# Expert parts with their last three tiles behind a branch, and parts of 3, 3 and 2 blocks behind attention

## The chip, the cores and the metric

The kernel runs on one core of one Trainium2 chip. A core has five engines that run side by side, each through its own instruction queue in order: TensorE (PE, matrix products), VectorE (DVE), ScalarE (ACT), GpSimd (POOL) and SyncE (SP, which here issues transfers). Engines wait for one another by semaphores. On-chip memory is SBUF, with PSUM as the target of matrix products; transfers between it and the large memory (HBM) are done by DMA, issued from the queues of SP, ACT and POOL.

The metric is the device time of one execution in microseconds (us). Before the change it is 656.89 us, the median of three runs (655.76 to 658.45).

## The reference

The input x is 16 sequences of 256 tokens with 128 features, float32. The layer is a feed-forward half, attention, and the same feed-forward half again:

```python
x = x + 0.5 * ffn(layernorm(x))
x = x + attention(layernorm(x))     # 16 heads of 8, causal
x = x + 0.5 * ffn(layernorm(x))
```

The feed-forward part is a mixture of experts. A token takes the two best of eight experts by a softmax over `layernorm(x) @ gate_w.T`, with the two weights scaled to sum to one. The reference computes every expert for every token and weights the unused ones with zero:

```python
weights, idx = top_k(softmax(flat @ gate_w.T), 2)
h1 = einsum("nd,ehd->neh", flat, w1); h3 = einsum("nd,ehd->neh", flat, w3)
y = einsum("neh,edh->ned", silu(h1) * h3, w2)     # 8 experts, 256 hidden units
out = einsum("ned,ne->nd", y, combine)
```

## The kernel before

**Blocks, parts and tiles.** The 4096 tokens are 8 blocks of 512, and a block is two sequences. Each feed-forward half is cut into three parts of whole blocks: 1, 3 and 4 blocks before attention (`ahead`), and 4, 3 and 1 behind it (`after`). The rows that a part sends to experts are sorted by expert into a scratch array in HBM (`part.x`), with every expert's rows starting at a multiple of 128. A tile is 128 such rows, all of one expert. A part of `blocks` blocks has `8 * blocks` tiles' worth of rows, and rounding up eight experts can add at most 7, so the kernel always works through `nj = 2 * ht + NE - 1` tiles, which is 15, 23, 31 or 39 for 1, 2, 3 or 4 blocks. That is 85 tiles before attention and 85 behind it. Tiles that hold no row are computed all the same. Three scratch pairs (`places`), for 1, 3 and 4 blocks, are used by both halves.

**Routing** (`route_in_steps`) finds on VectorE, from the gate's logits, the two experts of each token, counts tokens for each expert by a small matrix product, and yields the row of each token (`rowi`, L416), the expert of each tile (`eji`, L434), and the weights `c`. It is written as a generator, whose steps the caller spreads between other work.

**Scatter and gather.** `scatter` (L449) writes normalised rows to `part.x` with indirect DMAs from POOL, two for 128 tokens, so 8 for a block. `combine` (L611) reads the results back from `part.y` with as many indirect DMAs from POOL, and VectorE adds each to x (L602), at most some four transfers later. When a block is complete behind attention, SP stores it (`store`).

**The tile loop** (`experts`). For each group of three tiles SP loads rows (`xg`), two groups ahead, with three buffers; PE transposes them (`px`, L493), and ACT copies them to SBUF (`xgT`, L495). For each tile VectorE copies the expert's weights to a fixed place (`wt`, L502), two tiles ahead, by an address in a register that was loaded from `eji`. PE then makes four products to `ph` (L514), ACT applies silu (L525), VectorE multiplies (L536), and two tiles later PE makes two products to `py` (L544). For each group ACT copies `py` to `yg` (L554) and issues its store to `part.y`.

**The order of the work** is written out by hand: within `manual_schedule` each engine gets its instructions in program order. `experts_of` runs the tiles of one part. At every tile it takes `pulls` steps from `aside` (work on PE, ACT and VectorE that belongs to something else) and, from tile 2 on, `rate` steps from `beside` (scatters or gathers), each behind a small POOL memset called `tick`. When all tiles are begun it exhausts `aside`, with `ahead` also `beside`, and then fetches and begins the next part (its first loads, transposes and weight copies), before the last products of its own part. At the end it exhausts `beside`.

- Before attention: part one runs beside the scatters of part two and the norms, gates and routing of part three; part two beside the scatters of part three; part three beside the gathers of parts one and two and, from tile 14 on, the opening steps of attention.
- In attention, each batch (sequence) has eight steps `p`. At each, one step is taken from `moves`: first the gathers of the last part ahead (one in two steps), then the scatters of whichever part behind attention has been routed. When a sequence is finished, `finish` projects it and adds it to x, and after every second one normalises the block and computes its logits. With the last block of a part the routing follows, and its scatters join `moves`. In the last batch the first part behind attention begins, with five tiles (silu by tanh there).
- Behind attention: part one runs beside the rest of the scatters, and takes the rest of `finish` and the routing one step a tile (`ending`); part two beside the gathers of part one (one a tile); part three beside the gathers of part two (four in three tiles); and at last the gathers of part three.

Of the kernel before, what the change touches and what calls it, by code (L numbers as in the profile page):

```python
# [11 lines left out]
FP = mybir.dt.float32  # L12
BF = mybir.dt.bfloat16
I32 = mybir.dt.int32
AF = mybir.ActivationFunctionType
ALU = mybir.AluOpType
# [3 lines left out]
P = 128  # L20
NB, SEQ, D = 16, 256, 128
NH, DK = 16, 8
NE, NHID = 8, 256
# [12 lines left out]
HT = NT // 2  # L36
JG = 3
NJG = 13


class InTurn:
# [9 lines left out]
class Part:  # L51


    def __init__(self, first, blocks, scratch):
        self.first, self.blocks = first, blocks
        self.ht = blocks * TPB


        self.nj = 2 * self.ht + NE - 1
        self.ng = -(-self.nj // JG)  # L60
        self.x, self.y = scratch


MASKED = -1e30
# [3 lines left out]
def macaron_kernel(  # L68
# [41 lines left out]
    def load_x(*blocks):  # L110
        for t in blocks:
            nc.sync.dma_start(
                out=xs[t], in_=x[ts(t, BLK), :].rearrange("(c p) d -> p c d", p=P)
            )


    def scratch(name, blocks):
        rows = Part(0, blocks, (None, None)).nj * P
        return tuple(tc.dram_tile([rows, D], FP, name=f"{name}_{s}") for s in "xy")

    places = [scratch(f"rows{i}", n) for i, n in enumerate((1, 3, 4))]
    ZW = 16
    zeros = const.tile([P, ZW * D], FP)
    nc.vector.memset(zeros, 0.0)

    def clear(i, queue=nc.sync):
        rows = places[i][0].rearrange("(p c) d -> p (c d)", p=P)
        n = rows.shape[1]
        for at in range(0, n, ZW * D):
            w = min(ZW * D, n - at)  # L130
            queue.dma_start(out=rows[:, at : at + w], in_=zeros[:, 0:w])
# [1 line left out]
    gw_sb = const.tile([D, NE], FP)  # L133
    nc.scalar.dma_start(out=gw_sb, in_=gate_w)
    load_x(0, 1)
    clear(0)
    load_x(2, 3)
    w13_sb = const.tile([D, NE, 2, NHID], FP)
    w2_sb = const.tile([P, NHC, NE, D], FP)
# [4 lines left out]
    nc.sync.dma_start(out=w2_sb, in_=w2)  # L144
    clear(1)
    load_x(4, 5, 6, 7)
    wq_in = const.tile([D, NG, 4, 32], FP)
    wk_in = const.tile([D, NG, 4, 32], FP)
    wv_sb = const.tile([D, D], FP)
# [33 lines left out]
    nc.vector.memset(zero8, 0.0)  # L183

    goes_on = {}
    for blocks in (1, 3, 4):
        n = blocks * TPB
        go = const.tile([P, NE, n], FP, tag=f"goes_on{n}", name=f"goes_on{n}")
        nc.gpsimd.memset(go.rearrange("p e t -> p (e t)"), 1.0)
        nc.gpsimd.memset(go[:, :, 0], 0.0)  # L190
        goes_on[n] = go.rearrange("p e t -> p (e t)")
# [138 lines left out]
    def route_in_steps(part, ps, fine=False, placed_at=None):  # L330
# [86 lines left out]
        if placed_at is not None:  # L417
            placed_at(rowi)
        yield

        grid = [1, part.ng * 4, NE]
        past = work.tile([1, NJG * 4, NE], FP, tag="g_past", name="past")[:, 0 : part.ng * 4, :]
        nc.vector.tensor_tensor(
            past,
            jgrid[:, 0 : part.ng * 4, :],
            upto[0:1, :].unsqueeze(1).to_broadcast(grid),
            ALU.is_ge,
        )
        if fine:
            yield  # L430
        ej = work.tile([1, NJG * 4], FP, tag="g_ej", name="ej")[:, 0 : part.ng * 4]
        nc.vector.tensor_reduce(ej, past, AX.X, ALU.add)
        eji = work.tile([1, NJG * 4], I32, tag="g_eji", name="eji", bufs=3)
        nc.vector.tensor_scalar(eji[:, 0 : part.ng * 4], ej, float(NE - 1), None, ALU.min)  # L434

        den = new("den", [P, ht])
        nc.vector.tensor_scalar(den, ex, 2.0, 2.0, ALU.mult, ALU.add)
# [28 lines left out]
    def experts(part, eji):  # L466
# [71 lines left out]
        def project(j):  # L538
# [12 lines left out]
            if c == tiles(g) - 1:  # L551
# [7 lines left out]
                    in_=yg[:, 0:n, :],  # L559
                )  # L560

        def fetch():
            load(0)
            load(1)
# [23 lines left out]
                    project(j - 2)  # L588
                yield

        made = SimpleNamespace(part=part, fetch=fetch, begin=begin, tiles=run(), begun=False, by_tanh=False)
        return made


# [60 lines left out]
    def experts_of(  # L655
        work,
        beside,
        aside=iter(()),
        side=(0, 0),
        pulls=lambda j: 1,  # L660
        rate=lambda j: 1,
        then=None,
        opened=None,
        ahead=True,
    ):

        following = None

        def transfer():
            nc.gpsimd.memset(tick, 0.0)  # L674
            return next(beside, done)

        done = object()
        with opened or ExitStack() as stack:
            one = 1 if side[1] else 2
            if opened is None:  # L680
                banks = expert_banks(stack, one, 3 if side[1] else 4)
            else:
                banks = work.banks
                more = psum(stack, "ps_h2", 2)
                banks.h = InTurn(banks.h, more)
            if side[0]:
                pools["first"], pools["banks"] = psum(stack, "ps_f", 1), side[0]
            if side[1]:
                pools["side"] = psum(stack, "ps_m", side[1])
            stack.enter_context(manual())  # L690
            if not work.begun:
                work.fetch()
                work.begin(banks)
            work.banks = banks
            for _ in work.tiles:
                j = work.at
                for _ in range(pulls(j)):
                    next(aside, None)
                for _ in range(rate(j) if j >= 2 else 0):
                    transfer()  # L700
                if j == work.part.nj:
                    for _ in aside:
                        pass
                    while ahead and transfer() is not done:
                        pass
                    if then is not None:
                        following = then()
                        following.fetch()
                        following.begin(banks)
            while transfer() is not done:  # L710
                pass
        return following

# [319 lines left out]
        return opening, steps, routes, moves  # L1033

    ahead = [Part(0, 1, places[0]), Part(1, 3, places[1]), Part(4, 4, places[2])]
    after = [Part(0, 4, places[2]), Part(4, 3, places[1]), Part(7, 1, places[0])]


    stats, xns, xnTs, routes = {}, {}, {}, []
# [124 lines left out]
    def others():  # L1164
        part = ahead[2]
        blocks = range(part.first, part.first + part.blocks)
        for s in range(part.blocks + 2):
            t = part.first + s
            if t in blocks:
                normed(t)  # L1170
            if t + 2 in blocks:
                stats[t + 2] = moments(t + 2)
            if t - 1 in blocks:
                xnTs[t - 1] = transposed(t - 1, xns[t - 1], pools["side"])
            if t - 2 in blocks:
                gate_logits(t - 2, xnTs[t - 2], pools["side"])
            if s == part.blocks:
                clear(2, nc.scalar)
            yield
        routes.append((yield from route_in_steps(part, pools["side"])))  # L1180

# [10 lines left out]
    def back(part, route, after_block):  # L1192
        return combine(part, route[0], route[2], after_block)

    def store(t):
# [24 lines left out]
        itertools.chain(back(ahead[0], routes[0], none), back(ahead[1], routes[1], none)),  # L1220
        opening(),
        (2, 1),
        pulls=lambda j: int(j >= 14),
    )

    left, right = ExitStack(), ExitStack()
# [20 lines left out]
    with manual():  # L1247
# [10 lines left out]
        then=lambda: experts(after[1], left_routes[1][1]),  # L1258
        opened=opened,
    )  # L1260
    tiles = experts_of(
        tiles,
        back(after[0], left_routes[0], store),
        then=lambda: experts(after[2], left_routes[2][1]),
        ahead=False,
    )
    experts_of(
        tiles,
        back(after[1], left_routes[1], store),
        rate=lambda j: 1 + (j % 3 == 0),  # L1270
        ahead=False,
    )
    for _ in back(after[2], left_routes[2], store):
# [41 lines left out]
```

## Time and profile before

| | us |
|---|---|
| median of three runs | 656.89 |
| the profiled execution's own time | 657.1 |
| its span | 655.1 |
| PE busy | 576.9 (88%) |
| DVE busy | 448.2 (68%) |
| POOL busy | 419.7 (64%) |
| ACT busy | 352.7 (54%) |
| `ph` products (L514), 1360 records | 184.9 |
| `py` products (L544), 680 records | 104.6 |
| scatters (L449), 128 | 126.5 |
| gathers (L611), 128 | 124.9 |

The span is the time from the first to the last instruction of one profiled execution, and all times in a profile are counted from its start. A profile lists groups of instructions by line, with busy time, the mean of one in ns, and the idle time of the engine just before them with what ended it ("<-"). "issue" there is time in which the engine waited for nothing that the profile shows, such as the loading of registers. PE is a matrix product and PEld the load of its weights. The chain of work is followed back from the last instruction, at each step to what released it.

### The profile page before, as it was taken

What the parts mean: (1) busy time and instruction counts of PE and PEld (TensorE: products, weight loads), DVE (VectorE), ACT (ScalarE), POOL (GpSimd) and SP (SyncE); (2) the same over time, 40 slices, a digit from 0 to 9 for tenths busy, and PEclk for the clock granted to TensorE, in tenths of its full rate; (3) what the DMA queues carried; (4) which work ended last, traced back from release to release, by engine and by line L of the source; (5) the groups of instructions that cost most, each with busy time, mean ns of one, the idle gap of its engine ahead of it and who ended that gap; (6) DMA issues with size and microseconds to landing.
All of it is one profiled execution on the core that took longest, in us unless ns stands there. A gap on an engine that the chain in (4) does not pass through costs nothing.

```text
span 655.1 us, 17006 instructions
## 1 busy us (share of the span) xinstructions
PE 576.9 (88%) x6158; PEld 484.4 (74%) x6158; DVE 448.2 (68%) x1405; ACT 352.7 (54%) x730; POOL 419.7 (64%) x862
## 2 busy tenths in 40 slices
PE   4369799999998999999999999999998799999930
PEld 3258699999986677777777766777677799999930
DVE  7754765566665788888887899677646556576742
ACT  6245444446623667777686866675646345444410
POOL 3568889767532666666663437788710884787785
PEclk9989999999996999999999999999999979999985
DMA  8726444454310000000000000000112333456442
GB/s 301 276 86 225 131 125 130 134 137 107 78 42 20 19 14 20 18 18 15 18 18 3 2 2 23 29 30 36 58 38 60 110 110 94 131 148 165 122 121 72
DMA packets 65905, 53.73 MB, mean 82 GB/s; under 512 B 6560, under 2 KB 60576, under 8 KB 65312
## 3 DMA queue, kind: packets, MB, share of 16 engines
q1 hardware_dynamic: 34368, 22.16, 10.8%
q0 software_dynamic: 8192, 16.79, 8.6%
q10 hardware_dynamic: 23264, 13.71, 7.1%
q8 instruction: 50, 0.82, 0.5%
q14 instruction: 31, 0.25, 0.1%
HBM read 25.43 MB, written 27.20 MB: 80 GB/s over the span
## 4 chain that ended last, share of the span: by engine, by line
PE 70%; POOL 8%; DVE 8%; issue 5%; ACT 5%; DMA 2%; DVEq 1%; ACTq 0%; POOLq 0%; SPq 0%
PE ph L514 18%; PE sm L782 12%; PE py L544 8%; PE o L887 7%; PE sw L797 6%; PE sm L809 6%; POOL rows_x L449 4%; PE pl L315 3%; POOL yt L611 3%; PE px L493 2%; PE pt L302 2%; DVE top L813 2%; ACT pT L823 1%; PE pm L868 1%; PE po L925 1%
## 5 line engine op out<-in xcount | busy, mean ns | idle before, releaser
L514 PE MATMUL ph<-xgT,wt 128*128 128x128 f32 x1360 | 184.9, 280 | 8.6 <-DVE wt L502 6.7
L514 PEld LDWEIGHTS ph<-xgT,wt 128*128 128x128 f32 x1360 | 169.3, 196 | 11.7 <-DVE wt L502 5.5
L825 POOL TENSOR_SCALAR_AFFINE_SELECT pT<-pT 128x256 f32<-128x256 f32 x256 | 100.0, 414 | 107.4 <-ACT pT L823 106.3
L813 DVE TENSOR_REDUCE top<-sm 128x3 f32<-128x384 f32 x256 | 130.3, 551 | 54.5 <-PE sm L809 51.4
L449 POOL DMA_INDIRECT rows_x<-xn,rowi x128 | 126.5, 988 | 47.7 <-issue 22.6
L823 ACT ACTIVATE pT<-sw 128x768 f32<-128x768 f32 x128 | 104.0, 812 | 86.2 <-PE sw L797 79.3
L611 POOL DMA_INDIRECT yt<-rows_y,rowi x128 | 124.9, 975 | 28.4 <-issue 15.9
L782 PE MATMUL sm<-kp,qp 32*128 32x256 f32 (+1 forms) x1024 | 127.9, 354 | 3.2 <-ACT kp L758 1.6
L525 ACT ACTIVATE gt<-ph 128x256 f32<-128x256 f32 x165 | 63.2, 384 | 117.4 <-PE ph L514 108.1
L797 PE MATMUL sw<-qm,kp 32*128 32x128 f32 (+1 forms) x1024 | 120.9, 354 | 1.1 <-ACT pT L823 1.1
L782 PEld LDWEIGHTS sm<-kp,qp 32*128 32x128 f32 x1024 | 95.1, 187 | 31.3 <-DVE top L813 10.6
L536 DVE TENSOR_TENSOR gt<-gt,ph 128x256 f32<-128x256 f32 x165 | 68.6, 416 | 59.9 <-ACT gt L525 59.2
L544 PE MATMUL py<-w_sb,gt 128*128 x680 | 104.6, 278 | 3.3 <-ACT yg L554 1.9
L502 DVE COPY wt<-w_sb 128x512 f32 x170 | 75.7, 448 | 36.1 <-issue 25.0
L544 PEld LDWEIGHTS py<-w_sb,gt 128*128 128x128 f32 x680 | 90.5, 194 | 4.1 <-ACT yg L554 2.3
L797 PEld LDWEIGHTS sw<-qm,kp 32*128 32x128 f32 x1024 | 68.6, 189 | 2.8 <-ACT pT L823 1.8
L602 DVE SCALAR_TENSOR_TENSOR x<-yt,c,x 128x128 f32<-128x128 f32 x128 | 45.7, 361 | 18.3 <-DMA yt<-rows_y,rowi 18.0
L887 PE MATMUL o<-pT,vaug 128*32 128x256 f32 (+1 forms) x1024 | 56.2, 335 | 0.0
L809 PE MATMUL sm<-mask_two,ident_b 128*128 128x256 bf16 x256 | 50.8, 281 | 0.0
L250 POOL TENSOR_TENSOR rstd<-ve,neg_half 128x4 f32<-128x4 f32 x24 | 25.3, 1054 | 39.6 <-DVE ve L248 38.7
L887 PEld LDWEIGHTS o<-pT,vaug 128*32 128x32 f32 x1024 | 27.7, 110 | 23.2 <-issue 9.6
L674 POOL MEMSET tick<- 128x1 f32 x269 | 37.3, 139 | 5.7
(124 smaller groups left out, 660.3 us busy)
## 6 DMA issues: line engine op xcount, KB each, us to landing
xg<-rows_x SPq DMA_DIRECT2D x56, 192.0 KB, 2.9
rows_y<-yg ACTq DMA_DIRECT2D x56, 192.0 KB, 2.1
w_sb<-in_w SPq DMA_DIRECT2D x3, 1024.0 KB
x<-in_x SPq DMA_DIRECT2D x8, 256.0 KB, 13.8
rows_x<-xn,rowi POOLq DMA_INDIRECT x128
rows_x<-zeros ACTq DMA_DIRECT2D x2, 1024.0 KB
yt<-rows_y,rowi POOLq DMA_INDIRECT x128
out_y<-x SPq DMA_DIRECT2D x8, 256.0 KB, 3.5
```

Of the source, the lines that this page charges most:

```text
L449: i = nc.gpsimd.indirect_dma_start(out=part.x, out_offset=bass.IndirectOffsetOnAxis(ap=rowi[:, n, t : t + 1], axis=0), in_=xns[part.first ...
L502: nc.vector.tensor_copy(wt.rearrange("d k h -> d (k h)"), w13_f[:, bass.ds(es[g][c] * (2 * NHID), 2 * NHID)],)
L514: nc.tensor.matmul(out=ph[:, k // NHC, k % NHC, :], lhsT=wt[:, k, :], rhs=xTs[g][:, c, :], start=True, stop=True,)
L544: nc.tensor.matmul(out=ys[g][:, c, :], lhsT=gt[:, hc, :], rhs=w2_f[:, bass.ds(es[g][c] * D + hc * (NE * D), D)], start=(hc == 0), stop=(hc ...
L611: nc.gpsimd.indirect_dma_start(out=yt, out_offset=None, in_=part.y, in_offset=bass.IndirectOffsetOnAxis(ap=rowi[:, n, t : t + 1], axis=0),)
L782: nc.tensor.matmul(out=s[u][:, to], lhsT=qp[r, j, ts(q, P)], rhs=kp[r, SET[j], k], start=(q == 1), stop=False,)
L797: nc.tensor.matmul(out=s[:, u, to], lhsT=kp[r, SET[j], ts(k, P)], rhs=qm[r, j, q], start=True, stop=True,)
L809: nc.tensor.matmul(out=s[u][:, 128:384], lhsT=ident_b, rhs=mask_qk, start=False, stop=True)
L813: nc.vector.tensor_reduce(tops[b % 2][:, j, i0 + u, :], s[u][:, 0:384].rearrange("p (n k) -> p n k", k=P), AX.X, ALU.max,)
L823: nc.scalar.activation(pT, s[:, :, 0:384], AF.Exp, scale=DK**-0.5)
L825: nc.gpsimd.affine_select(out=pT[:, u, 0:256].rearrange("p (n q) -> p n q", q=P), in_=pT[:, u, 0:256].rearrange("p (n q) -> p n q", q=P), ...
L887: nc.tensor.matmul(out=o[32 * i : 32 * i + 32, j // 2, q], lhsT=va[:, kt, 4 * j + i, :], rhs=pTs[i // 2][:, i % 2, at], start=(j % 2 == 0 ...
```

## The change

A part now always computes `nj = most - 3` tiles, where `most` is the former bound: 12, 20, 28 and 36 for 1, 2, 3 and 4 blocks. The three remaining tiles stand in `rest`, behind a branch. Every engine loads the number of tiles that the routing counted into a register, and the body is entered only if it exceeds `nj`. The body does load, transposes, products and store of three tiles one after the other. It stands behind all other tiles of its part, so behind the first loads, transposes and weight copies of the next one. What the three tiles' rows of `part.y` hold otherwise are zeros, which four new transfers from SP write near the start.

Behind attention the parts have 3, 3 and 2 blocks in place of 4, 3 and 1. So the scratch for one block becomes one for two, and a further transfer on ACT's queue clears its rest. Before attention there are now 12 + 28 + 36 = 76 tiles outside branches, and behind it 28 + 28 + 20 = 76.

Three constants follow: the opening of attention is taken from tile 11 on, the gathers beside the last part are five in four tiles, and gathers of the first part that are left when the second part's tiles end are carried on beside the third part.

```diff
@@ class Part
-        self.nj = 2 * self.ht + NE - 1
+        self.most = 2 * self.ht + NE - 1
+        self.nj = self.most - SPARE
         self.ng = -(-self.nj // JG)
+        self.grid = -(-self.most // JG)
+        self.x, self.y = (s[: self.most * P] if s is not None else None for s in scratch)
@@ macaron_kernel
-    places = [scratch(f"rows{i}", n) for i, n in enumerate((1, 3, 4))]
+    places = [scratch(f"rows{i}", n) for i, n in enumerate((2, 3, 4))]
...
-    clear(0)
+    clear(0, upto=at_first)
...
     load_x(4, 5, 6, 7)
+    for part in (Part(0, n, places[i]) for i, n in ((0, 1), (0, 2), (1, 3), (2, 4))):
+        nc.sync.dma_start(
+            out=part.y[part.nj * P :, :].rearrange("(p c) d -> p c d", p=P),
+            in_=zeros[:, 0 : SPARE * D],
+        )
...
-    for blocks in (1, 3, 4):
+    for blocks in (1, 2, 3, 4):
@@ route_in_steps
+        nc.vector.tensor_copy(eji[:, NJG * 4 : NJG * 4 + 1], upto[0:1, NE - 1 : NE])
@@ experts
+        def rest():
+            counted = nc.values_load(
+                eji[0:1, NJG * 4 : NJG * 4 + 1],
+                min_val=0,
+                max_val=part.most,
+                skip_runtime_bounds_check_because="tiles are counted by the routing",
+            )
+            banks = made.banks
+            few = range(part.nj, part.most)
+            rows = slice(part.nj * P, part.most * P)
+            with tc.If(counted > part.nj):
+                xg = work.tile([P, JG, D], FP, tag="xg", name="xg", bufs=3)
+                nc.sync.dma_start(
+                    out=xg, in_=part.x[rows, :].rearrange("(c p) d -> p c d", p=P)
+                )
+                px = banks.x.tile([P, JG, P], FP, tag="x", name="px")
+                for c in range(SPARE):
+                    nc.tensor.transpose(px[:, c, :], xg[:, c, :], ident)
+                xT = work.tile([D, JG, P], FP, tag="xgT", name="xgT", bufs=2)
+                nc.scalar.copy(xT, px)
+                wt = work.tile([D, SPARE, 2 * NHC, P], FP, tag="w_rest", name="w_rest", bufs=1)
+                py = banks.y.tile([P, JG, D], FP, tag="y", name="py")
+                for c, j in enumerate(few):
...
+                yg = work.tile([P, JG, D], FP, tag="yg", name="yg", bufs=3)
+                nc.scalar.copy(yg, py)
+                nc.scalar.dma_start(
+                    out=part.y[rows, :].rearrange("(c p) d -> p c d", p=P), in_=yg
+                )
@@ experts_of
-            while transfer() is not done:
+            work.rest()
+            while all_of_them and transfer() is not done:
                 pass
@@ the parts
-    after = [Part(0, 4, places[2]), Part(4, 3, places[1]), Part(7, 1, places[0])]
+    after = [Part(0, 3, places[1]), Part(3, 3, places[2]), Part(6, 2, places[0])]
@@ others
                 clear(2, nc.scalar)
+                clear(0, nc.scalar, since=at_first)
@@ the calls of experts_of
-        pulls=lambda j: int(j >= 14),
+        pulls=lambda j: int(j >= 11),
...
+    gathers = back(after[0], left_routes[0], store)
     tiles = experts_of(
         tiles,
-        back(after[0], left_routes[0], store),
+        gathers,
         then=lambda: experts(after[2], left_routes[2][1]),
         ahead=False,
+        all_of_them=False,
     )
     experts_of(
         tiles,
-        back(after[1], left_routes[1], store),
-        rate=lambda j: 1 + (j % 3 == 0),
+        itertools.chain(gathers, back(after[1], left_routes[1], store)),
+        rate=lambda j: 1 + (j % 4 == 0),
         ahead=False,
     )
```

## The prediction

> **What bounds the kernel now.** I read the page's chain of work first, then the busy time by stretch, then the timelines of POOL, PE and DVE around the ends of the parts. The chain by engine:
>
> ```profile
> PE 70%; POOL 8%; DVE 8%; issue 5%; ACT 5%; DMA 2%; DVEq 1%; ACTq 0%; POOLq 0%; SPq 0%
> ```
>
> TensorE carries it, and POOL only in places. The stretches say where (PE busy, count, PEld, DVE, ACT, POOL, then granted clock, DMA share, GB/s):
>
> ```profile
> 34.00:79.00 45.00, 35.20 (x248) 31.22 (x248) 26.23 (x105) 22.73 (x50) 33.85 (x70) 0.96 0.41 140
> 79.00:125.00 46.00, 45.28 (x402) 45.01 (x403) 26.64 (x90) 20.87 (x53) 40.03 (x107) 1.00 0.44 133
> 125.00:205.00 80.00, 76.87 (x636) 71.23 (x636) 51.85 (x151) 38.80 (x95) 41.04 (x88) 0.97 0.33 88
> 205.00:475.00 270.00, 265.18 (x3588) 190.99 (x3586) 215.68 (x621) 182.72 (x343) 171.84 (x323) 0.99 0.07 20
> 475.00:556.00 81.00, 71.89 (x623) 67.03 (x623) 46.72 (x163) 40.04 (x83) 40.55 (x86) 0.95 0.27 83
> 618.00:655.00 37.00, 10.27 (x90) 9.89 (x88) 13.99 (x41) 4.55 (x11) 26.11 (x44) 0.70 0.36 96
> ```
>
> PE is nearly full from 79 to 618 us, has holes before 79 and from 475 to 556, and does little in the last 37 us, where POOL's gathers run alone. POOL's timeline gives the tail its joints:
>
> ```profile
> 119.58 5.72 POOL L674 MEMSET tick<- 128x1 f32 x33
> ...
> 506.93 1.03 POOL L449 DMA_INDIRECT rows_x<-xn,rowi  x1 [14.66 <-DVE rowi L416]
> ...
> 548.64 1.35 POOL L449 DMA_INDIRECT rows_x<-xn,rowi  x1 [7.19 <-ACT yg L554]
> ...
> 563.87 1.06 POOL L611 DMA_INDIRECT yt<-rows_y,rowi  x1 [1.59 <-DMA xg<-rows_x]
> ...
> 609.42 1.04 POOL L611 DMA_INDIRECT yt<-rows_y,rowi  x1 [2.50 <-DVE wt L502]
> ...
> 648.57 0.95 POOL L611 DMA_INDIRECT yt<-rows_y,rowi  x1 [0.30 <-issue]
> ```
>
> Scatters of the 3-block part start at 506.9, those of the last block at 548.6, the 64 gathers at 563.9; the 33rd, first of the second part, waits until 609.4 for its rows. Then 32 follow without a hole, (648.57-609.42)/31 = 1.26 us each, and the span ends 6.5 us after the last starts.
>
> **What a tile costs.** L514 and L544 leave 8, 4 and (L493) 1 matmul records per tile. Between 79 and 124 us a group of three tiles takes 4.35 us, so 1.45 us each. The work removed is 170 - 152 = 18 tiles, 26 us of PE if nothing else sets the pace. Routing the reference's own inputs (top two of eight, counts divided by 128 and rounded up) gives 12, 27 and 35 tiles for the parts before attention against bounds of 12, 28 and 36, and 28, 28 and 19 against 28, 28 and 20 behind it. No branch should be entered; three counts lie on the bound.
>
> **Before attention.** Part one, 15 to 12 tiles: its PE work ends near 76, but the next part's ph starts at 79.1, released by POOL's 24th scatter (72.0 plus its 1 us), 2.2 us of landing and a 3.2 us load. Scatters run 1.27 us apart from 50 us whatever PE does: gain 0. Part two, 31 to 28: the 32 scatters of the next part fill POOL from 76.1 to 119.6, and this wait already stands in front of the next part:
>
> ```profile
> 124.30 0.55 PE L493 MATMUL px<-ident,xg 128*128 128x128 f32 x3 [0.63 <-DMA xg<-rows_x]
> ```
>
> PE would come 4.35 us sooner and wait as much longer. Fewer idle ticks on POOL may give 1 us, a register load there takes it: 0. Part three, 39 to 36, holds attention's opening, one step a tile over 25 tiles both before (from tile 14) and after (from 11). The eight rows of block 0 are added by 142.5 us, its moments start at 147.0; three tiles earlier is 142.6. It just fits: 3 x 1.45 = 4.3 us gained, 0 if those adds come late.
>
> Small additions: four 192 KB stores of zeros on SP, by ACT's issue row (0.37 us) 1.5 us, stand before the first xg load, which waits for scatters until 31 us; one more clear on ACT (0.4 us, in a stretch where ACT is half idle); two POOL memsets (0.3 us, before a 2.3 us wait); six copies of 0.17 us on DVE. 0 each, and at most 2 us together if that cover were gone.
>
> **Attention.** The second part is now complete after block 5, so its routing and 9 of its 24 scatters move inside; 8 scatters of the first part leave. DVE gains some 6 us of short operations where it is busy 216 of 270 us: 0, at worst +3.
>
> **Behind attention.** Steps for the last block are taken one a tile. Before, eight routing steps of the 3-block part went first (tiles 5 to 12), and the last block's began with the reciprocal at 509.9; after, they begin at tile 5, near 495.7: 14.2 us sooner. Its rstd also stood behind twelve scatters on POOL:
>
> ```profile
> 523.20 0.16 DVE L255 SCALAR_TENSOR_TENSOR less<-mv,rstd 128x4 f32<-128x4 f32 x1 [4.93 <-POOL rstd L250]
> ...
> 547.73 0.17 DVE L416 CAST rowi<-rows 128x8 int32<-128x8 f32 x1
> ```
>
> With part of these scatters inside attention I take 1 of the 4.9 us as left. So rowi comes at 547.9 - 14.2 - 3.9 = 530. Then 16 scatters, not 8: 16 x 1.27 = 20 us, POOL free at 550.5 (before 558.9), first gather 551.5.
>
> PE: 23 tiles from 494.6 at 1.45 = 33.3, plus 8.4 of the 14.3 us of extra work and stalls that the 34 tiles had (3.9 of rstd and 2 of one pair of exp table loads go): 536.3, first ph of the second part 538 and a branch. Its adds on DVE wait for the gathers from tile 7 on: gate 27 stands behind add 20, 551.5 + 20 x 1.26 + 3.3 = 580, so its last product is at 582.5 and its rows land at 585.5 (copy 0.5, issue 0.4, landing 2.1). POOL, done with 24 gathers at 582, waits until 586. The third part: ph at 585 with branch and start, 20 x 1.45 to 614, landed 618; POOL's 24 gathers end at 616. The last 16 start at 619 with the branch, the last at 619 + 15 x 1.26 = 637.8, end 644.3: 10.8 us sooner. The gain is smaller than PE's because 16 rather than 8 gathers now follow the last tile, 10 us more.
>
> **The branch.** No row shows one. Each needs a register on every engine, then the joining of counts behind it. Queued behind it on PE are the next part's ph, on DVE wt and gt, on ACT gt and xgT, on SP the third load, on POOL the next transfers. Nearest row: registers for three tiles before a weight copy,
>
> ```profile
> L502 DVE COPY wt<-w_sb 128x512 f32 x170 | 75.7, 448 | 36.1 <-issue 25.0
> ```
>
> 25.0 us over 38 waits, 0.66 each. Low end 0.5 us, as PE's queue hides part. High end: the join also waits for a store and a load in flight, 0.7 + 2.1 + 2.9 = 5.7. A gain is excluded, since it only adds. I take 1.5, one register load and one hand-over between PE and ACT (0.6 to 0.8), near the low end. Six places, the last counted 1.0: 8.5 us, of which 4.5 lie before attention and 4.0 are in the tail's joints.
>
> Here a rule of the Trainium skill speaks against the change: "Runtime: NRT & Kernel Launch", section "Instruction fetch mechanics", says that a taken branch whose target is outside the two fetched blocks of 256 instructions stalls for a fetch. The row:
>
> ```profile
> q8 instruction: 50, 0.82, 0.5%
> ```
>
> 0.82 MB / 50 is 16.4 KB a packet, as that page has it, but no branch is in the trace. The longest body, PE's, has 3 x 13 matmuls with as many loads, about 90 instructions: one block ahead at most. I charge nothing; if each jump did refetch, at about the 2.9 us of an xg load, six would add 17 us and the sum would end slower, at 664.
>
> **Sum.** 655.1 - 4.3 + 4.5 - 10.8 = 644.5 us of span. The profiled execution took 657.1, 2.0 above its span; the median of the runs is 656.9. So 646.4, called 646.
>
> **Rivals.**
> Cheap joins: all six at 0.5 give 646.4 - 5.5 = 641, and rstd without a stall 640. For it: PE's gaps marked issue are 0.3 to 0.6 us. Against: the buffers used in the branch rotate into the next part.
> POOL takes it back: if the last block's steps are not sooner (rowi still at 548), 16 scatters end at 568.5, the last of 64 gathers starts 63 x 1.26 = 79.4 after the first, and the end is 568.5 + 1 + 79.4 + 6.5 + 0.2 (from before attention) = 655.6, median 657: no change. For it: the steps wait on three engines at 2.1 us a tile. Against: the eight steps ahead of them are gone by the order of the code.
> The join drains: each branch waits for DMAs in flight. Without branches the sum is 636.0, so 19.1 us are to be lost: from 3.2 us a branch it is slower. At 5.7 the span is 670, median 672. For it: a store of y is in flight at every branch. Against: it is awaited by later gathers only, if the counts are joined engine by engine.
> The branch is entered: load, transposes, three tiles in series and the store, some 12 us each. The counts exclude it unless a token flips at a bound; the nearest count below a multiple of 128, where the total is on its bound, is 124: four tokens to spare.
>
> **Chances.** As forecast (639 to 653) 0.56; cheap joins 0.12; POOL takes it back 0.12; the join drains 0.18; entered 0.02. The range 638 to 664 leaves out some 0.05 below and 0.12 above; that of the likeliest alone is 639 to 653. A change under 0.5% (3.3 us) can't be told from none: faster 0.68, same 0.12, slower 0.20.
>
> **What would show it.** ph count 1216 in place of 1360; ph of part two near 79 to 81 and of part three near 125 to 127 (no gain there); rowi of the last part some 35 us after the first tile behind attention, with 16 scatters directly behind it; POOL holes of some 4 and 2 us before the gathers of parts two and three; 16 gathers behind the last tile. At each branch a PE hole under 2 us. Holes of 3 us or more, or gathers that start after 565, make the prediction wrong.

## The result, and the profile after

The changed kernel takes 664.37 us, the median of four runs (662.46 to 665.02), against 656.49 for the kernel before beside it (655.76 to 658.45). The ratio is 1.010, with a 95% interval of 1.006 to 1.014: slower by 1%, where 646 and faster were forecast. The profiled execution took 664.98, 1.7 us more than its span of 663.3.

The chain of work of the changed kernel breaks off near its end, so it can't be set beside the one shown of before:

```profile
DMA 2%; issue 1%; POOL 1%; DVE 0%; POOLq 0%; DVEq 0%
```

The busy times by stretch can. Those of the changed kernel (columns as before the change: PE busy, count, PEld, DVE, ACT, POOL, granted clock, DMA share, GB/s):

```profile
34.00:79.00 45.00, 31.70 (x214) 28.26 (x215) 25.57 (x107) 19.52 (x44) 36.67 (x70) 0.93 0.45 158
79.00:125.00 46.00, 43.95 (x373) 43.79 (x372) 24.27 (x86) 20.87 (x50) 39.10 (x104) 0.95 0.41 125
125.00:205.00 80.00, 76.31 (x599) 68.01 (x598) 48.98 (x146) 36.38 (x88) 37.13 (x71) 0.93 0.28 76
205.00:475.00 270.00, 262.15 (x3542) 188.61 (x3542) 217.14 (x647) 178.99 (x338) 165.06 (x315) 0.99 0.06 19
475.00:556.00 81.00, 73.08 (x597) 63.30 (x596) 40.75 (x130) 37.87 (x81) 43.94 (x92) 0.89 0.26 78
618.00:663.00 45.00, 12.32 (x105) 11.69 (x103) 16.41 (x48) 5.57 (x14) 31.59 (x47) 0.66 0.34 94
```

Up to 475 us little differs. From 475 to 556 PE counts as busier than before, 73.08 against 71.89 us, and yet works off fewer products (597 against 623) at a lower clock (0.89 against 0.95). So the loss is near the end of attention. The products `o`, weights times values, are the last of each of its batches. Their row has shortest, median and longest duration in ns, then first and last start. Before:

```profile
L887 PE MATMUL o<-pT,vaug x1024: 272/379/637, 209.7 to 493.0; 128*32 128x256 f32 x86, 128*32 128x128 f32 x85
```

After:

```profile
L966 PE MATMUL o<-pT,vaug x1024: 272/379/637, 207.4 to 505.6; 128*32 128x128 f32 x86, 128*32 128x256 f32 x85
```

This cuts the difference of the two spans into three. Attention's first `o` comes 2.3 us sooner; from its first `o` to its last it takes 298.2 us in place of 283.3, 14.9 more; from the last `o` to the end it is 663.3 - 505.6 = 157.7 in place of 655.1 - 493.0 = 162.1, 4.4 less. -2.3 + 14.9 - 4.4 = 8.2, the difference of the spans. So the stretch of attention, which the forecast put at nothing, lost about twice what the rest gained. (A second profile of the kernel before has its `o` from 211.6 to 493.4 us, so a joint of one profile can move by 2 us.)

POOL's timeline in the last batch (start, duration, engine and line, then the idle time before it and what ended it) shows why:

```profile
464.40 0.77 POOL L904 TENSOR_SCALAR_AFFINE_SELECT pT<-pT 128x256 f32<-128x256 f32 x2 [1.15 <-ACT pT L902]
466.99 1.02 POOL L462 DMA_INDIRECT rows_x<-xn,rowi  x1 [1.82 <-DVE rowi L426]
468.02 0.12 POOL L752 MEMSET tick<- 128x1 f32 x1
468.32 0.97 POOL L462 DMA_INDIRECT rows_x<-xn,rowi  x1 [0.18 <-issue]
469.29 0.12 POOL L752 MEMSET tick<- 128x1 f32 x1
469.60 0.97 POOL L462 DMA_INDIRECT rows_x<-xn,rowi  x1 [0.19 <-issue]
470.56 0.12 POOL L752 MEMSET tick<- 128x1 f32 x1
470.87 0.97 POOL L462 DMA_INDIRECT rows_x<-xn,rowi  x1 [0.19 <-issue]
471.85 0.78 POOL L904 TENSOR_SCALAR_AFFINE_SELECT pT<-pT 128x256 f32<-128x256 f32 x2
```

L904 is the select that masks attention's weights `pT`, and PE's `o` needs it. Four scatters stand between two pairs of selects that follow one another in attention. The ticks tell whose they are: the tile loop behind attention sets one for each of its scatters (`transfer` in `experts_of`), attention's own have none. (The tick of the first of the four had run already, before attention.) In program order these scatters come after every select of attention. But here the order written out by hand held only within one region of it (one `manual_schedule`). Attention is one region, the tile loop behind it is another, and the scatters needed nothing but `rowi` of the second part, which now exists at 466.5 because blocks 3 to 5 are complete by then. From 466.99 to 481.9 POOL took eight scatters of the later loop, four, three and one of them, ahead of three pairs of selects that PE waits for. In PE's timeline:

```profile
472.33 1.84 PE L966 MATMUL o<-pT,vaug 128*32 128x256 f32 x12 [4.07 <-POOL pT L904]
479.15 1.42 PE L966 MATMUL o<-pT,vaug 128*32 128x256 f32 x4 [0.75 <-POOL pT L904]
482.37 1.84 PE L966 MATMUL o<-pT,vaug 128*32 128x256 f32 x12 [1.80 <-POOL pT L904]
```

After the first of these waits TensorE's products are slower, too. From 472 to 492 us the granted clock is 0.51, and 76 products are worked off; with the eight scatters held back (below) it is 1.00 there, and there are 184. Eight products `sw` of attention, in the changed kernel and then with the scatters held back:

```profile
474.10 1.65 PE L876 MATMUL sw<-qm,kp 32*128 32x128 f32 x8
```

```profile
482.15 0.92 PE L880 MATMUL sw<-qm,kp 32*128 32x128 f32 x8
```

Behind attention POOL's timeline has these joints, in the changed kernel:

```profile
541.27 0.97 POOL L462 DMA_INDIRECT rows_x<-xn,rowi  x1 [10.16 <-DVE rowi L426]
...
563.94 0.98 POOL L688 DMA_INDIRECT yt<-rows_y,rowi  x1 [1.20 <-issue]
...
603.84 1.14 POOL L688 DMA_INDIRECT yt<-rows_y,rowi  x1 [8.65 <-DVE gt L549]
...
637.84 0.95 POOL L688 DMA_INDIRECT yt<-rows_y,rowi  x1 [0.86 <-DVE x L679]
```

The 16 scatters of the last part start at 541.3, the gathers of part one at 563.9, of part two at 603.8 and of part three at 637.8; the last of them starts at 656.7.

No branch body was entered: `ph` has 1216 records, and the packets of the instruction queue are as many as before (`q8 instruction: 50`). The compare-and-branch instructions of the six branches and the semaphores behind them are on line 586 (queue, operation, shortest/median/longest ns):

```profile
L586 PEldq EVENT_SEMAPHORE  x12: 51/51/51, 76.0 to 632.0; - x12
L586 POOLq COMPARE_BRANCH  x6: 45/45/45, 71.7 to 636.0; - x6
L586 SPq COMPARE_BRANCH  x6: 45/45/50, 73.0 to 629.4; - x6
L586 DVEq COMPARE_BRANCH  x6: 56/56/72, 74.0 to 638.8; - x6
L586 PEldq COMPARE_BRANCH  x6: 210/233/342, 74.9 to 631.6; - x6
L586 ACTq COMPARE_BRANCH  x6: 45/45/45, 77.6 to 632.7; - x6
...
  PE ph L527: 8.0, 4
...
  PE px L506: 5.4, 1
```

The last two lines are who waited: the first `ph` behind a branch, 8.0 us in four places, and once `px`, 5.4 us.

### The profile page after: what moved, and what is told of

Its sections match the earlier page's. It is cut to its first block, busy times and chain, and to the rows that moved or that the text cites. A ratio compares the mean times of both kernels' runs of the same rounds, so it can differ in the third digit from the quotient of the medians.

```text
span 663.3 us, 16469 instructions
## 1 busy us (share of the span) xinstructions
PE 565.2 (85%) x5924; PEld 466.2 (70%) x5924; DVE 433.1 (65%) x1375; ACT 337.5 (51%) x700; POOL 413.8 (62%) x827
## 5 line engine op out<-in xcount | busy, mean ns | idle before, releaser
L527 PE MATMUL ph<-xgT,wt 128*128 128x128 f32 x1216 | 170.0, 286 | 18.1 <-DVE wt L515 9.4
L527 PEld LDWEIGHTS ph<-xgT,wt 128*128 128x128 f32 x1216 | 156.0, 201 | 21.8 <-ACTq L586 8.8
L904 POOL TENSOR_SCALAR_AFFINE_SELECT pT<-pT 128x256 f32<-128x256 f32 x256 | 99.8, 414 | 112.5 <-ACT pT L902 111.5
L876 PE MATMUL sw<-qm,kp 32*128 32x128 f32 (+1 forms) x1024 | 123.3, 360 | 1.1 <-ACT pT L902 0.6
L538 ACT ACTIVATE gt<-ph 128x256 f32<-128x256 f32 x147 | 56.1, 383 | 121.3 <-PE ph L527 111.9
L861 PEld LDWEIGHTS sm<-kp,qp 32*128 32x128 f32 x1024 | 94.8, 187 | 31.3 <-DVE top L892 10.2
L549 DVE TENSOR_TENSOR gt<-gt,ph 128x256 f32<-128x256 f32 x147 | 61.2, 416 | 59.8 <-ACT gt L538 59.2
L557 PE MATMUL py<-w_sb,gt 128*128 x608 | 93.6, 278 | 2.1 <-DVE gt L549 2.0
L515 DVE COPY wt<-w_sb 128x512 f32 x152 | 67.0, 444 | 34.7 <-issue 25.0
L557 PEld LDWEIGHTS py<-w_sb,gt 128*128 128x128 f32 x608 | 80.9, 194 | 2.7 <-DVE gt L549 2.7
L966 PE MATMUL o<-pT,vaug 128*32 128x256 f32 (+1 forms) x1024 | 60.0, 340 | 6.6 <-POOL pT L904 6.6
L506 PE MATMUL px<-ident,xg 128*128 128x128 f32 x152 | 28.4, 298 | 11.4 <-SPq L586 5.4
(125 smaller groups left out, 653.6 us busy)
```

What stands on the lines that cost most here:

```text
L515: nc.vector.tensor_copy(wt.rearrange("d k h -> d (k h)"), w13_f[:, bass.ds(es[g][c] * (2 * NHID), 2 * NHID)],)
L527: nc.tensor.matmul(out=ph[:, k // NHC, k % NHC, :], lhsT=wt[:, k, :], rhs=xTs[g][:, c, :], start=True, stop=True,)
L549: nc.vector.tensor_tensor(gt, gt, ph[:, 1], ALU.mult)
L557: nc.tensor.matmul(out=ys[g][:, c, :], lhsT=gt[:, hc, :], rhs=w2_f[:, bass.ds(es[g][c] * D + hc * (NE * D), D)], start=(hc == 0), stop=(hc ...
L861: nc.tensor.matmul(out=s[u][:, to], lhsT=qp[r, j, ts(q, P)], rhs=kp[r, SET[j], k], start=(q == 1), stop=False,)
L876: nc.tensor.matmul(out=s[:, u, to], lhsT=kp[r, SET[j], ts(k, P)], rhs=qm[r, j, q], start=True, stop=True,)
```

## The experiments

Theory H: the eight scatters of the later loop, drawn ahead of attention's last selects, cost the time. Rival B: the branches and their joins do. Rival S: the parts of 3, 3 and 2 do, by the 16 gathers behind the last tile.

In twelve of the eighteen runs the surroundings were others: the kernel before itself took 768 to 781 us beside them. In those profiles TensorE stands still in the tile loops while POOL goes on. The changed kernel there, in three stretches of 8 us:

```profile
108.00:116.00 8.00, 3.41 (x25) 2.97 (x25) 2.04 (x11) 0.61 (x2) 6.93 (x13) 0.93 0.23 80
116.00:124.00 8.00, 2.02 (x7) 1.76 (x7) 0.00 (x0) 0.00 (x0) 6.85 (x13) 0.50 0.13 52
124.00:132.00 8.00, 0.37 (x1) 0.00 (x0) 0.30 (x1) 0.38 (x1) 5.25 (x17) 0.50 0.10 41
```

Seven products from 116 to 124; the first profile of the same kernel has 74 from 108 to 116. The profile puts the gaps between them to "issue", that is to nothing it shows, and what caused them stays open; chip 0 is listed for runs of both kinds. So these twelve are compared only with one another, by ratio and by the attention stretch, where they differ little. The other six (called calm here: the three named `..._calm`, `before_here`, `held_late` and `late_no_branch`) stand beside a kernel before of 657 to 658 us and carry the sizes.

**Holding back the eight scatters.** One POOL instruction ahead of the tiles behind attention reads attention's last `pT`; nothing on PE, DVE, ACT and SP changes its place.

```diff
@@ attention
+    ended_with = []
...
+            ended_with.append(last[0][-1])
@@ experts_of
             stack.enter_context(manual())
+            if opened is not None:
+                nc.gpsimd.tensor_copy(tick, ended_with[0][:, 1, 128:129])
             if not work.begun:
```

> The changed kernel, with one POOL copy of 128x1 ahead of the tiles behind attention that reads attention's last pT. So the tick and scatters of the tile loop behind attention can't stand before attention's last selects on POOL; attention's own nine scatters stay, the order on PE, DVE, ACT and SP is the same. Scatters ahead of the selects stretch the last batch: its last o comes near 493 in place of 505, and all after it 11 to 13 us sooner, time 651 to 654. If branches or the parts of 3, 3 and 2 are the cause, the last batch's gain is lost again at the joints and it stays at 661 to 665.

> The changed kernel as it is, beside the next three on one chip. 1.01 times the kernel before, as in the result; last select of attention some 302 us behind the first (287 before).

> The same kernel as the run held, on another chip, since that one's holes on ACT and PE were not those of the profiles before and after. Scatters as the cause: attention's selects span 287 to 290 us, the time is 11 to 13 us under the changed kernel's, ratio to before 0.992 to 0.996. Otherwise 1.005 to 1.01.

> The kernel of the run held once more, on a chip of its own turn: in the earlier runs of it TensorE's products in the tile loops came with gaps of 1 to 2 us that the profiles of before and after don't have. Without these gaps and with scatters as the cause: attention's selects span 287 to 290 us and the ratio to before is 0.992 to 0.996, time 651 to 654; with the scatters no cause 1.005 to 1.01. With these gaps again: near 0.982 as before.

> The kernel of the run held, where the kernel before takes 657. Only the eight scatters of the later tile loop are kept behind attention, the nine of attention's own stay in its last batch. If the eight carried the loss: first o to last o 285 to 287 us, time 650 to 653. If the nine of its own cost as much: 653 to 658, and held_late's 650 is owed to both.

| | us | before beside it | ratio (95%) | first to last `o` |
|---|---|---|---|---|
| held | 755.46 | 771.04 | 0.982 (0.975 to 0.988) | 289.6 |
| after_again | 772.89 | 780.90 | 0.989 (0.982 to 0.996) | 303.2 |
| held_again | 764.95 | 780.90 | 0.982 (0.977 to 0.986) | 290.6 |
| held_third | 755.54 | 768.42 | 0.986 (0.976 to 0.997) | 289.9 |
| held_calm | 650.48 | 658.05 | 0.990 (0.986 to 0.993) | 284.2 |

In calm surroundings holding eight scatters back takes the change from 664.4 to 650.5 us, and from slower to faster than before. That is 13.9 us by the medians, 2.0% by the ratios, and in the profiles the attention stretch falls from 298.2 to 284.2. Held keeps the branches and the parts, so neither B nor S makes this difference. In the other surroundings the stretch falls by nearly as much, from 303.2 to 290.6 on one chip. Held_calm's row of `o`:

```profile
L970 PE MATMUL o<-pT,vaug x1024: 272/379/636, 207.5 to 491.7; 128*32 128x256 f32 x87, 128*32 128x128 f32 x84
```

And its POOL timeline at the end of attention:

```profile
487.41 0.98 POOL L462 DMA_INDIRECT rows_x<-xn,rowi  x1 [0.17 <-issue]
490.14 0.94 POOL L908 TENSOR_SCALAR_AFFINE_SELECT pT<-pT 128x256 f32<-128x256 f32 x2 [1.75 <-ACT pT L906]
491.25 0.98 POOL L462 DMA_INDIRECT rows_x<-xn,rowi  x1 [0.16 <-issue]
492.24 0.20 POOL L770 COPY tick<-pT 128x1 f32<-128x1 f32 x1
492.50 0.10 POOL L752 MEMSET tick<- 128x1 f32 x1
492.75 0.99 POOL L462 DMA_INDIRECT rows_x<-xn,rowi  x1
```

The first scatter with a tick now comes at 492.75, behind the last select and the added copy. It costs nothing to have them later: they run where POOL would wait for the next `rowi` anyway (10.16 us in the changed kernel).

One thing the expectations did not have: in the other surroundings the changed kernel is faster than before (0.989), though the scatters delay attention by the same 13 us. The kernel before takes 112 to 124 us more there, while held's attention stretch takes only some 6 more (284.2 to 290). If the rest lies with the 170 tiles, it is some 0.6 us for each, and 18 fewer tiles save 11 us more. This is argued, not shown: no profile of the kernel before was taken there.

**The nine scatters of attention's own.** As held, and attention takes no step of `moves` in its last batch.

```diff
-                    next(moves[0], None)
+                    if b < NB - 1:
+                        next(moves[0], None)
```

> As held, and the nine scatters of attention's own that its last batch took from the second part behind attention also wait until the last select is through. If these nine delay the selects as well, the stretch from the first o to the last falls from 290 to 283 to 286 us and the time by up to 5 us; if they cost nothing there, the stretch stays at 290 and the time rises by 0 to 9 us, since nine scatters at 1.27 us come later.

It took 650.05 us against 657.26, ratio 0.990 (0.985 to 0.994), with 204.9 to 489.2 for `o`, a stretch of 284.3. Held_calm has 284.2: the nine cost nothing, as forecast. (The 290 in the expectation came from the other surroundings.) It also beats both kernels.

**Without branches.** `work.rest()` is taken out; the last three tiles of each part are left out altogether, with the scatters placed as in the changed kernel (no_branch), as in held (held_no_branch) and as in held_late (late_no_branch).

```diff
-            work.rest()
```

> The changed kernel without its six branches; three tiles at the end of each part are left out altogether (the routing of this input fills none of them). Scatters as the cause: only the price of the branches goes, six at about 2 us of PE, of which those at attention's start and behind the last tile cost little: 654 to 658. If branches and their joins are the cause of the loss (drain of the queues, later gathers): 640 to 648. If a branch is hidden: 663 to 665.

> The same kernel as the run no_branch: the changed kernel without its branches (three tiles at the end of each part are left out; scatters still ahead of the selects). Scatters as the main cause: 6 to 12 us under the changed kernel, ratio to before 0.993 to 1.002, with attention still 302 us long. If the branches cost more than my 8.5 us, below 0.99.

> As held, and without the six branches (three tiles at the end of each part left out altogether). Without the gaps: 8 to 12 us under held if six branches cost about 2 us each on the path, 641 to 645, ratio 0.978 to 0.983; 8.5 us was my own price. If the branches are hidden: as held. If the branches are dearer than their holes: below 0.975.

> The kernel of the run no_branch (six branches gone, three tiles at the end of each part left out, scatters still ahead of the selects). Against 664.4 for the changed kernel: my price of 8.5 us for six branches gives 656; branches as the main cause would give 650 or less; free branches 664.

> As held_late, and without the branches (the last three tiles of each part are left out altogether). Against held_late's 650: 640 to 644 if the six cost the 8.5 us of the forecast or what their holes of 2 us show, 645 to 648 if part of the holes is made good later.

| | us | ratio (95%) | first, last `o`, stretch | last `o` to span end |
|---|---|---|---|---|
| no_branch | 756.07 | 0.982 (0.974 to 0.990) | 262.0, 564.9, 302.9 | 188.8 |
| no_branch_again | 767.18 | 0.983 (0.978 to 0.988) | 268.9, 572.0, 303.1 | 192.9 |
| held_no_branch | 750.90 | 0.980 (0.969 to 0.990) | 263.1, 553.0, 289.9 | 194.4 |
| no_branch_calm | 656.99 | 1.000 (0.996 to 1.003) | 200.4, 497.6, 297.2 | 154.6 |
| late_no_branch | 640.10 | 0.974 (0.970 to 0.977) | 200.7, 483.2, 282.5 | 155.1 |

Late_no_branch's `o`:

```profile
L969 PE MATMUL o<-pT,vaug x1024: 272/326/636, 200.7 to 483.2; 128*32 128x256 f32 x86, 128*32 128x128 f32 x85
```

Without branches but with the scatters ahead, the kernel is as slow as before: 297.2 us in attention. So B alone doesn't explain the loss, and in calm surroundings the two causes add up; in the others held_no_branch (0.980) can't be told from held_third (0.986) on the same chip. These sizes are rough, for the ten runs of no_branch_calm go from 653.6 to 664.8. By the medians six branches cost 664.4 - 657.0 = 7.4 us in one pair and 650.05 - 640.10 = 10.0 in the other, by the spans 663.3 - 652.2 = 11.1 and 646.1 - 638.3 = 7.8: between 7 and 11. Of this, the three ahead of attention take 4.2 (204.9 against 200.7) to 7.0 (207.4 against 200.4), the stretch of attention 1.0 to 1.8, and the three behind it 1.8 (156.9 against 155.1) to 3.1 (157.7 against 154.6).

**The branch without the new parts.** Parts of 4, 3 and 1 behind attention, with `rate` as before the change; the gathers left over by the second part go on beside the third, as in the changed kernel. (The sizes of the scratch arrays and what clears them follow.)

```diff
-    after = [Part(0, 3, places[1]), Part(3, 3, places[2]), Part(6, 2, places[0])]
+    after = [Part(0, 4, places[2]), Part(4, 3, places[1]), Part(7, 1, places[0])]
```

> Three tiles of each part behind a branch, but parts of 4, 3 and 1 blocks behind attention as before the change; the 3-block part is then routed behind attention and no scatters can be drawn ahead of the selects. Scatters as the cause: last o back at 492 to 493, 18 tiles fewer and six branches, 645 to 650. If the branches are the cause: 660 or more, slower than before. If the parts of 3, 3 and 2 with 16 gathers behind the last tile are the cause by themselves: 640 to 650 too, so this run only sets the branch apart.

> The same kernel as the run branch_431: branches, but parts of 4, 3 and 1 behind attention. Scatters as the cause: attention 287 to 290 us long, ratio to before 0.98 to 0.992. If the branches were the cause: 1.0 or more.

> The kernel of the run branch_431 (branches, parts of 4, 3 and 1). With the scatters as the cause nothing delays attention: first o to last o 283 to 285 us, time 646 to 651, ratio 0.983 to 0.992. With the branches as the cause: 657 or more.

758.80 against 771.04 (0.989, 0.979 to 0.998), 767.51 against 780.90 (0.982, 0.977 to 0.986), and calm 654.91 against 658.05 (0.995, 0.992 to 0.998). With the 3-block part routed behind attention again there is nothing to draw ahead, and the calm stretch from first to last `o` is 282.6 (207.7 to 490.3): again H and not B. The time is above the expected 646 to 651; its ten runs go from 650.3 to 662.5, and its profiled one was 650.3, as short as held_calm's 650.0. By the medians the parts of 3, 3 and 2, held, are 4.4 us better than 4, 3 and 1 with the same branches; so wide a spread leaves this size open.

**The new parts without the branch.** All tiles computed, no branch, no stores of zeros; opening steps from tile 14 as before. First with the scatters ahead, then held.

```diff
-        self.nj = self.most - SPARE
+        self.nj = self.most
```

> Parts of 3, 3 and 2 blocks behind attention without the branch and with all tiles computed as before the change (no stores of zeros either). Scatters as the cause: they are drawn ahead here too, last o 12 us later than before, and with 8 more gathers behind the last tile and no tile saved 668 to 680. If the branches are the cause: near 657.

> Parts of 3, 3 and 2 behind attention, all tiles computed, no branch, and the scatters of the later tile loop kept behind attention's selects as in held. Against late_no_branch's 640 it shows what 18 tiles save: my forecast has 4.3 before attention and 18 to 22 in all with the split's 16 gathers at the end paid, so 656 to 664. If parts of 3, 3 and 2 are better by themselves than 4, 3 and 1: below 656, under the kernel before with the same number of tiles.

780.43 against 771.04, ratio 1.012 (1.003 to 1.020), with 300.1 us from first to last `o`; and, held, 772.16 against 767.83, ratio 1.005 (1.002 to 1.008), with 289.0. The parts alone, without any branch, lose 1.2%. Holding the scatters takes back 11 us of the stretch; the 0.7 points between the ratios lie within their intervals. So the stretch leads to the same reading a third way. Both fell into the other surroundings, so the microseconds expected can't be compared; the ratios say that the parts of 3, 3 and 2 gain nothing by themselves, and that held's 0.982 to 0.986 there comes from the tiles saved.

**Four branches.** As held; the first two parts ahead of attention compute all their tiles and have no branch.

```diff
-    ahead = [Part(0, 1, places[0]), Part(1, 3, places[1]), Part(4, 4, places[2])]
+    ahead = [Part(0, 1, places[0], 0), Part(1, 3, places[1], 0), Part(4, 4, places[2])]
```

> As held (650.5), but the first two parts before attention compute all their tiles, 15 and 31, and have no branch; four branches are left. My forecast gave the six tiles saved there no gain and their branches 3 us together: then 646 to 649. If the tiles saved there pay for the branches, as the starts of parts two and three 1.3 and 2.1 us earlier say: 651 to 655.

763.54 against 767.83, ratio 0.996 (0.992 to 1.000), where held has 0.982, 0.982 and 0.986 in such surroundings. There the six tiles are worth more than the two branches cost. In calm surroundings this kernel was not run.

**The kernel before once more.**

> The kernel before itself, for its profile in the surroundings of the experiments, where every kernel takes some 100 us longer than in the first profiles. If the extra time falls evenly on the tiles of the tile loops, it is 100/170, some 0.6 us a tile, and the 18 tiles that the change removes save 10 us more here than there; the attention stretch stays at 283 to 285 us from the first o to the last (303 in the changed kernel here, 290 when the scatters are held).

It took 657.24 against 657.26 for its own twin, 1.001 (0.998 to 1.003), with a span of 654.8: the surroundings had changed back, so it gave no profile of the kernel before among the gaps. Two sets of runs of the same kernel differ here by 0.1%, with an interval of up to 0.3%.

## Why the prediction was wrong, point by point

**The step that failed** is "Attention": "its routing and 9 of its 24 scatters move inside; 8 scatters of the first part leave", priced "0, at worst +3" by DVE's load alone. The nine cost nothing (held_late), and with the eight held back the stretch with its routing is 284.2 us, against 283.3 and 281.8 in the two profiles of the kernel before. But 17 scatters moved inside, not 9: eight more from the next region, which POOL took ahead of selects that PE was waiting for. The price was 14.9 us in the profiles, and 13.9 when held back. Eight scatters with their ticks are 8 x 1.27 = 10.2 us of POOL. What stood behind them came later as well: DVE's `less` waited 5.65 us for `rstd` on POOL until 476.16, and its `rc` 9.55 for PE's `pq` until 487.70. And TensorE worked at a granted clock of 0.51 from 472 to 492. How the 14.9 us divide between waiting and slower products stays open. The forecast looked at which steps attention takes, and not at what in the next region had just become ready.

**The rest of the sum held up.** With the eight held back, against the forecast's own joints:

| | forecast | held_calm |
|---|---|---|
| `rowi` of the last part | 530 | 526.9 |
| first `ph` of part two | 538 | 534.5 |
| first gather | 551.5 | 550.0 |
| first gather of part two | 586 | 589.7 |
| first of the last 16 gathers | 619 | 622.9 |
| last gather | 637.8 | 641.6 |
| span end | 644.3 | 648.3 |

```profile
550.02 0.99 POOL L688 DMA_INDIRECT yt<-rows_y,rowi  x1 [1.09 <-issue]
...
589.65 0.94 POOL L688 DMA_INDIRECT yt<-rows_y,rowi  x1 [8.49 <-DMA xg<-rows_x]
...
622.91 0.94 POOL L688 DMA_INDIRECT yt<-rows_y,rowi  x1 [0.86 <-DVE x L679]
```

The one joint that went wrong is part two: 39.6 us from the first gather to its own rows, forecast 34.5. PE's last product ended at 584.3 instead of 582.5. PE had stood still for 6.26 us until 553.44: it waited for weights that DVE copied behind its first add, and the add for its gather. Then 4.9 us in place of 2.5 passed from the issue of the last store (584.79) to the gather. The hole that POOL has there was forecast at 4 us and is 8.5; the next, forecast at 2, is 0.9. That the end is only 4.0 us off is in part luck, since the sooner start of attention makes up for some of this. The last part's `rowi` came 35 us behind attention's last `o` in the changed kernel (540.8 - 505.6) and in held_calm (526.9 - 491.7); the forecast has some 35 behind the first tile there.

**Before attention**, forecast +0.2: -4.3 for tiles and +4.5 for branches. Measured: without branches attention starts at 200.4 and 200.7 in place of 209.7, so the tiles are worth 9.1 us and not 4.3 (some 11 by the second profile of the kernel before, 211.6); the three branches take 4.2 to 7.0 of it. The net is -2.2 to -4.8. "Gain 0" for parts one and two was too low: both parts start sooner even with a branch in front, 77.8 against 79.1 and 123.3 against 125.4. For part one the premise failed that POOL's scatters stay where they are: the last of the row in front of that start comes at 69.24 in place of 72.01. Why it came sooner is open.

**The branch** was priced at 1.5 us a place and 8.5 in all; the runs say 7 to 11. The holes on PE in front of the first `ph` behind a branch are 1.81, 2.05, 1.87 and 2.30, where under 2 was forecast. One more hole is put down to a branch, and it is longer than the 3 us that were to prove the prediction wrong:

```profile
74.25 0.90 PE L506 MATMUL px<-ident,xg 128*128 128x128 f32 x3 [5.44 <-SPq L586]
```

But without branches PE waits there too, 4.64 us (no_branch_calm) and 4.71 (late_no_branch), for the load of `xg`, and the first `ph` then starts at 75.8 and 76.1 in place of 77.8. So of this hole and the 1.81 behind it some 2 us are the branch's. The prediction also weighed a rule of the Trainium skill ("Runtime: NRT & Kernel Launch", section "Instruction fetch mechanics"): a taken branch stalls for a fetch if its target lies outside the blocks already fetched. By the prediction's estimate six such stalls would have added 17 us. The 7 to 11 in all leave no room for that, and no run here shows a stall; the jump passes some 90 instructions at most, by the prediction's count. To charge nothing for it was right, and break-even, at 3.2 us a branch, was not reached.

**The rivals.** "The join drains" (672) is false: six branches cost 7 to 11 us in all, and not 5.7 each. The measured 664 also stands in the prediction, as the sum with a fetch at each jump; that it agrees is chance, for the time was lost elsewhere. "POOL takes it back" named POOL, but through the last block's steps, which came as far behind attention as forecast. The other sign that was to prove it wrong, "gathers that start after 565", did not appear (563.94), though attention's last `o` came 12.6 us later than before the change; that sign mixed the end of attention with what lies behind it.

## What to carry to other kernels

When a change makes an index or a buffer ready earlier, list every instruction that depends only on it, in later regions too, and see which queue they can now enter ahead of urgent work; here the hand-written order of one region didn't bind the next, and one small true dependence (a 0.20 us copy) did. Cut a difference of two traces at a row that both have, such as the first and last `o`, before any cause is named: a gain of 4.4, one of 2.3 and a loss of 14.9 looked like a change that loses 8. A branch that is never entered cost 1.2 to 1.8 us a place here, by the mean of six and about as much as one tile of 1.45 us, and must save more than that on the path.

## What the runs showed of the hardware

The compare-and-branch itself is short, 45 to 72 ns on four queues and 210 to 342 on PE's. The 2 us or so that PE stands still in front of a `ph` behind a branch must lie mostly elsewhere; the loading of registers and the handing over between engines around the branch are the likely places, but the profile does not list them apart.

Waits of 4.07, 0.75 and 1.80 us on PE went with a granted clock of 0.51 over 20 us, against 1.00 where the scatters were held back, and eight products `sw` took 1.65 us in place of 0.92.

The same kernel on the same inputs took 657 or 768 to 781 us. In the profiles of the longer kind, single products of TensorE stand 1.1 to 1.8 us apart for some 16 us at a time in the tile loops, at about the same places of the program, while POOL issues its scatters every 1.27 us throughout. The cause is open. In those surroundings this change comes out at 0.989 and not at 1.010.
